# Dense attention of a six-phase model: norm roots for four token tiles at once, scaling by ScalarE, and the norm's bias times the weights by one-column products

## The chip, the cores and the metric

The kernel runs on one core of a Trainium2 chip. A core has five engines, each with an instruction queue of its own that it works off in order: TensorE (PE in the profile; its weight loads are listed apart as PEld), VectorE (DVE), ScalarE (ACT), GpSimd (POOL) and SyncE (SP), which here only issues transfers. The metric is device time in microseconds. The kernel before was run three times: 3253.14, 3248.87 and 3249.95 us, a median of 3249.95 us.

## The reference

The input `x` is fp32 of shape (4, 1024, 128). Six phases follow each other, each added to `x`: a feed-forward, an attention by squared distances, the same feed-forward again, a windowed block (two layers, each a 64-token windowed attention of 8 heads and a gated part), the dense attention, and the windowed block again with the same weights.

```python
x = x + 0.5 * ffn(layernorm(x))           # phase ffn0a
x = x + l2_attention(layernorm(x))        # phase attn0
x = x + 0.5 * ffn(layernorm(x))           # phase ffn0b
x = x + 0.5 * windowed(layernorm(x))      # phase ffn1a
x = x + dense_attention(layernorm(x))     # phase attn1
x = x + 0.5 * windowed(layernorm(x))      # phase ffn1b
```

The change touches the dense attention alone. With 16 heads of 64 it computes, for every batch of 1024 tokens:

```python
mu, var = mean(x), var(x)                           # over the 128 features
xn  = (x - mu) / sqrt(var + 1e-05) * gamma + beta
q, k, v = split(xn @ w_qkv.T)                       # w_qkv is (3072, 128), no bias of its own
sim  = (q * 64 ** -0.5) @ k.T                       # per head, entries above the diagonal masked
out  = softmax(sim) @ v
y    = concat_heads(out) @ w_out.T + b_out
```

`x` comes to it through the layer norm without parameters of the line above, and it normalises again inside; the two norms are computed as one, with both epsilons in one root.

`xn @ w_qkv.T` splits into two parts: the normalised tokens times weights that have gamma multiplied in, and a constant of each output column, the sum over the features of `beta[d] * w_qkv[e, d]`. These 3072 constants are called the norm's bias times the weights below. gamma and beta are drawn at random, so neither is trivial.

## The kernel before

**Planner.** The kernel is not written in the order in which it runs. Each phase is a function that records small steps, each a closure of one or a few instructions, by `at(t, f)` with a nominal time `t`. A class `Plan` finds the dependencies between steps from the buffers that they touch, prices every step with a cost table, and lists the steps of each engine in an order: at each point an engine takes, of the steps that could start now, the one with the smallest priority (`order`). Buffers in SBUF and PSUM are placed in the same pass, and a step that opens a buffer waits until a place is free. From the result it works out the latest time of each step (`latest`), uses these as new priorities, and keeps the best of six such passes (`best_order`). Then the instructions are emitted, and each engine executes its list strictly in that order. So an edit of a few steps can reorder the work of neighbouring phases. All instructions carry line 237, that of the helper that issues them (`issue`).

**Phases.** `tile_macaron` records the six phases; each starts near the end of the one before and overlaps with it by as much as the planner finds room for. `attn1` (line 1087) gets its nominal start `T0`, and its preparation starts 40 nominal us ahead (`lead`). The preparation overlaps with the end of the windowed block.

**Dense attention.** A head pair (two heads of 64, together 128 columns) of one batch is the unit: 4 batches by 8 pairs are 32 pairs, n = 8b + p, each nominally 30.9 us. Its parts are:

- `load`, `mask`, `gain`, `load2` (lines 1097 to 1111): gamma, beta, the causal mask, gamma times 1/8, the output weights and bias. Beta is read as a row that is broadcast to 128 partitions.
- `weights(t, k)` (line 1113): the 3072 columns come in six blocks of 512, in the order 2, 0, 4, 3, 1, 5 (0 and 1 queries, 2 and 3 keys, 4 and 5 values); the last three are recorded 30 nominal us later, and are first needed by pair 4. `fetch` loads a block with features on partitions (`raw`, two buffers). `high` (ScalarE) multiplies it by gamma and rounds it to fp32r; `low` (DVE) makes the rest that the rounding left. For the bias, `fetch_rows` loads the same 512 columns a second time with the columns on partitions (`nat`, 256 KB), `times_bias` (POOL) multiplies by beta, and `total` (DVE) sums over the features into four columns of `bias`; for queries a further DVE step multiplies by 1/8.
- `norm(t0, w, b, t)` (line 1149), for each of the 8 token tiles of 128 of a batch: `stats` (two DVE instructions: mean and variance), `var` (DVE), the helper `rsqrt` (line 608: an integer estimate of 1/sqrt and two refinements, eight DVE instructions, here on one column), `scale` (DVE, 128x128), `bias_x` (POOL adds the output bias to x), `turn` (TensorE transposes the tile into PSUM), `upper` (ScalarE copies and rounds to fp32r) and `lower` (DVE, the rest). The first batch's eight norms are recorded in the preparation, 1.5 nominal us apart; those of batch b+1 one per pair while batch b is worked on.
- `project`: query and key projections of a pair, in two halves of 512 tokens. Each is three matmuls into PSUM (high times high, high times low, low times high), a ScalarE copy that adds the bias column (`upper`), a DVE subtraction (`lower`), and transfers that spread the two heads over separate tiles.
- `value`: the values of one token tile for four pairs, three matmuls and a DVE copy.
- `heads`: scores (four PSUM banks, 0 to 3), maximum (DVE), exp with its sum (ScalarE), reciprocal (DVE), normalising (POOL), transposing (TensorE, banks 4 and 5) and copying.
- `weigh`: probabilities times values (bank 6), the copy that adds the value bias, the output projection, and the addition to x.

All norm transposes, projections, values and output projections share one PSUM bank, number 7, under the name `wide`: each of them has to wait until its predecessor there is read.

In phases ffn0a, attn0 and ffn0b a different norm helper is used, `norm4` (line 644): statistics of four tiles, one root for the four columns, and the scaling of chosen tiles by ScalarE.

Of the kernel before, what the change touches and what calls it, by code (L numbers as in the profile page):

```python
# [14 lines left out]
AF = mybir.ActivationFunctionType  # L15
ALU = mybir.AluOpType
AX = mybir.AxisListType
# [4 lines left out]
EPS = 1e-5  # L22
# [69 lines left out]
class Plan:  # L92
# [22 lines left out]
    def at(self, t, f, *args):  # L115
        self.steps.append(Step(t, f, args))
# [478 lines left out]
class Macaron:  # L595
# [491 lines left out]
    def attn1(self, ph, T0, lead):  # L1087

        V, at, pe, ac, ve, gp, sy, tile_ = self.begin("a1.")
        a, plan = self.a, self.plan  # L1090
        W = {}
        T = 30.9
        wide = lambda: plan.bank("a1.m", [7], turns=False)
# [3 lines left out]
        def load():  # L1097
            W["gam"], W["gam8"], W["bet"] = tile_([128, 1], "gam"), tile_([128, 1], "gam8"), tile_([128, 128], "bet")
            W["bias"], W["cm"] = tile_([128, 24], "bias"), tile_([128, 128], "cm", 1, BF)
            sy.dma_start(out=W["gam"], in_=a["L1_attn_ln_gamma"].unsqueeze(1))  # L1100
            sy.dma_start(out=W["bet"], in_=a["L1_attn_ln_beta"].unsqueeze(0).broadcast_to([128, 128]))

# [11 lines left out]
        def weights(t, k):  # L1114
# [13 lines left out]

            def fetch_rows():
                W["nat", k] = tile_([128, 4, 128], "nat", 2)  # L1130
                rows = a["L1_attn_w_qkv"].rearrange("(c p) d -> p c d", p=128)
                sy.dma_start(out=W["nat", k], in_=rows[:, 4 * k : 4 * k + 4, :])

            def times_bias():
                gp.tensor_tensor(W["nat", k], W["nat", k], W["bet"].unsqueeze(1).broadcast_to([128, 4, 128]), ALU.mult)

            def total():
                o = W["bias"][:, 4 * k : 4 * k + 4]
                ve.tensor_reduce(o, W["nat", k], AX.X, ALU.add)
                if k < 2:  # L1140
                    ve.tensor_scalar(o, o, 0.125, None, ALU.mult)

            at(t, fetch)
            at(t + 0.1, fetch_rows)
            for j, f in enumerate((high, low, times_bias, total)):
                at(t + 3 + 0.5 * j, f)


        def norm(t0, w, b, t):
            x = lambda: self.X[2 * b + t // 4][:, t % 4, :]  # L1150
            K = ("ln", b, t)
            cs = slice(128 * (t % 4), 128 * (t % 4) + 128)

            def stats():
                s6, mv = tile_([128, 6], "s6", 3), tile_([128, 2], "mv", 3)
                V[K] = mv, tile_([128, 1], "lv", 3), tile_([128, 1], "ly", 3)
                ve.bn_stats(s6, x())
                ve.bn_aggr(mv, s6)

            def var():  # L1160
                mv, v, y = V[K]
                ve.tensor_scalar(v, mv[:, 1:2], 1.0 + EPS, EPS * EPS, ALU.mult, ALU.add)

            def scale():
                mv, v, y = V[K]
                V["xn", K] = tile_([128, D], "xn", 3)
                ve.tensor_scalar(V["xn", K], x(), mv[:, 0:1], y, ALU.subtract, ALU.mult)

# [234 lines left out]
        for t in range(8):  # L1403
            norm(tb + 5 + 1.5 * t, 2.0, 0, t)
        for t in range(8):
            value(T0 - 6.0 + 0.7 * t, 0, 0, t)
        work = [2 * (3.3 * (i + 1) + 2) for i in range(8)]
        for n in range(N):
# [6 lines left out]
            if b + 1 < self.B:  # L1415
                norm(t0 - 21.0, 8.0, b + 1, p)
            if n + 4 < N:
# [668 lines left out]
```

## Time and profile before

| quantity | value |
|---|---|
| median of three runs | 3249.95 us |
| the profiled execution's own time | 3244.27 us |
| its span (first to last instruction) | 3242.3 us |
| instructions | 76442 |
| mean granted TensorE clock | 0.984 |
| PE busy | 3033.2 us, 94% |
| PEld busy | 2128.3 us, 66% |
| DVE busy | 2237.5 us, 69% |
| ACT busy | 2455.6 us, 76% |
| POOL busy | 1461.8 us, 45% |
| transfers | 138.96 MB in 212596 packets, mean 43 GB/s |
| chain that ended last | PE 54%, DVE 17%, ACT 17%, issue 6%, POOL 5%, DMA 1%, SP queue 1% |

"Busy" is the time in which an engine had an instruction running; neighbouring instructions can overlap, so that the sum of single durations is longer than the time that they take. The chain that ended last is followed back from the last instruction of the program: at each step to what released it, or to the instruction before it on its engine. The granted clock is the share of full speed that TensorE was given. Since all instructions carry one line, groups are told apart by engine, operation, the program's buffer names (`words` and `wordsS` in SBUF, `wordsR` rounded fp32r tiles in SBUF, `wordsP` in PSUM) and by shape.

A few events of the time around the changed code, in us from the span's start: the last scores of the windowed attention on TensorE 1343.2; the transfers of gamma and beta issued 1343.8; the statistics of the first token tile of the dense attention 1345.5; the transposes of its eight tiles 1353.6 to 1375.5; the first key projection 1390.7; the first query projection 1404.3; the first scores of the dense attention 1412.1; the last work of the dense attention about 2536.

### The profile page before, as it was taken

How to read it: one execution, taken by the hardware profiler on the slowest of the kernel's cores; microseconds unless marked ns; L12 is line 12 of the kernel's file. 1: busy time of each engine (PE TensorE's matmuls, PEld its weight loads, DVE VectorE, ACT ScalarE, POOL GpSimd, SP SyncE). 2: the span in 40 equal slices, each digit the busy share in tenths (PEclk: the TensorE clock that was granted, in tenths of full speed). 3: DMA queues.
4: the chain of work that ended last, by engine and by line, in shares of the span. 5: the costliest groups of instructions: out<-in, count | busy, mean ns of one | idle time of the engine just before them, and what ended most of it. 6: DMA issues, size and time to landing. Idle time of an engine off the chain costs nothing.

```text
span 3242.3 us, 76442 instructions
## 1 busy us (share of the span) xinstructions
PE 3033.2 (94%) x27033; PEld 2128.3 (66%) x27060; DVE 2237.5 (69%) x6889; ACT 2455.6 (76%) x6818; POOL 1461.8 (45%) x1627
## 2 busy tenths in 40 slices
PE   8999999989998999889999999999999899999988
PEld 6322222667776777667777777777777677777767
DVE  8433341568767676788888888887787787676774
ACT  6999999778868686647767766777777788686873
POOL 1000000179958585433333333333343799585870
PEclk9999999999999999989999999999999999999999
DMA  1000000022212121222222121222231322122211
GB/s 40 1 1 1 1 3 11 25 69 64 55 39 59 44 56 31 52 67 46 47 52 45 42 51 42 45 48 52 45 84 35 75 56 58 37 59 46 57 42 30
DMA packets 212596, 138.96 MB, mean 43 GB/s; under 512 B 148516, under 2 KB 167800, under 8 KB 212216
## 3 DMA queue, kind: packets, MB, share of 16 engines
q1 hardware_dynamic: 211496, 133.51, 18.1%
q8 instruction: 217, 3.56, 0.5%
q14 instruction: 163, 1.34, 0.1%
q0 software_dynamic: 720, 0.56, 0.1%
HBM read 19.22 MB, written 2.10 MB: 7 GB/s over the span
## 4 chain that ended last, share of the span: by engine, by line
PE 54%; DVE 17%; ACT 17%; issue 6%; POOL 5%; DMA 1%; SPq 1%; DVEq 0%; ACTq 0%; POOLq 0%
PE wordsP L237 54%; ACT wordsS L237 12%; DVE wordsS L237 11%; DVE words L237 4%; POOL wordsS L237 4%; ACT words L237 4%; POOL words L237 1%; DVE wordsP L237 1%; DVE wordsR L237 1%; SPq L237 1%; ACT wordsR L237 0%; DMA wordsS<-wordsS 0%; ACT wordsP L237 0%; DMA words<-W_vT 0%; DMA words<-words 0%
## 5 line engine op out<-in xcount | busy, mean ns | idle before, releaser
L237 PE MATMUL wordsP<-wordsS 128*128 128x128 f32 (+7 forms) x12013 | 1653.3, 330 | 131.6 <-POOL wordsS L237 48.7
L237 ACT ACTIVATE wordsS<-wordsP,wordsS 128x128 f32<-128x128 f32 (+4 forms) x1952 | 920.8, 495 | 349.8 <-PE wordsP L237 211.0
L237 PEld LDWEIGHTS wordsP<-wordsS 128*128 128x128 f32 (+3 forms) x10248 | 916.2, 144 | 356.2 <-POOL wordsS L237 101.8
L237 POOL TENSOR_SCALAR wordsS<-wordsS 128x128 f32<-128x128 f32 (+7 forms) x630 | 478.0, 761 | 686.3 <-DVE wordsS L237 489.0
L237 PE MATMUL wordsP<-wordsR 128*128 128x512 f32 (+2 forms) x2592 | 725.9, 411 | 20.1 <-DVE wordsR L237 5.9
L237 POOL TENSOR_TENSOR wordsS<-wordsS 128x512 f32<-128x512 f32 (+1 forms) x518 | 541.5, 1060 | 445.4 <-DVE wordsS L237 422.1
L237 ACT COPY wordsS<-wordsP 128x512 f32<-128x512 f32 (+4 forms) x1040 | 543.2, 540 | 188.1 <-PE wordsP L237 181.0
L237 DVE TENSOR_REDUCE wordsS<-wordsP 128x1 f32<-128x512 f32 (+4 forms) x1024 | 576.4, 581 | 75.3 <-PE wordsP L237 68.8
L237 PE MATMUL wordsP<-wordsS,words 128*64 128x64 f32 (+3 forms) x6216 | 521.3, 298 | 32.3 <-DVE words L237 12.6
L237 PEld LDWEIGHTS wordsP<-wordsR 128*128 128x128 f32 (+1 forms) x2592 | 454.7, 192 | 124.0 <-ACT words L237 10.2
L237 ACT ACTIVATE wordsS<-wordsP 128x1024 f32<-128x1024 f32 (+3 forms) x640 | 515.7, 869 | 25.1 <-PE wordsP L237 20.7
L237 PE MATMUL wordsP<-words 128*128 128x512 f32 (+3 forms) x1540 | 418.1, 376 | 11.9 <-DMA words<-W_vT 10.6
L237 ACT ACTIVATION_READ_ACCUMULATOR wordsS<-wordsP,wordsS 128x1 f32 x1792 | 397.5, 222 | 0.0
L237 DVE COPY wordsS<-wordsP 128x512 f32<-128x512 f32 (+4 forms) x444 | 238.6, 550 | 211.0 <-PE wordsP L237 206.2
L237 PEld LDWEIGHTS <-wordsS 64*128 64x128 bf16 (+1 forms) x1792 | 117.9, 95 | 389.3 <-issue 372.2
L237 PEld LDWEIGHTS wordsP<-wordsS,words 128*64 128x64 f32 (+2 forms) x5704 | 300.4, 136 | 99.1 <-issue 47.5
L237 DVE TENSOR_TENSOR wordsS<-wordsP,wordsS 128x256 f32<-128x256 f32 (+3 forms) x560 | 251.9, 461 | 160.7 <-PE wordsP L237 123.1
L237 DVE TENSOR_TENSOR words<-wordsP,wordsS 128x256 f32<-128x256 f32 (+1 forms) x448 | 227.3, 526 | 129.8 <-PE wordsP L237 83.9
L237 PEld LDWEIGHTS wordsP<-words 128*128 128x128 f32 x1540 | 247.7, 192 | 43.4 <-DMA words<-W_kT 10.6
L237 PEld LDWEIGHTS wordsP<-words,wordsS 64*64 64x64 f32 (+1 forms) x4672 | 186.6, 142 | 78.3 <-issue 54.6
L237 PE MATMUL wordsP<-words,wordsS 64*64 64x128 f32 (+1 forms) x4672 | 227.2, 279 | 7.7 <-POOL words L237 2.7
L237 ACT ACTIVATE words<-wordsP,wordsS 128x512 fp32r<-128x512 f32 (+1 forms) x192 | 131.2, 690 | 73.3 <-PE wordsP L237 66.3
(62 smaller groups left out, 2263.7 us busy)
## 6 DMA issues: line engine op xcount, KB each, us to landing
words<-words SPq DMA_DIRECT2D x648, 128.0 KB
wordsS<-words SPq DMA_DIRECT2D x88, 128.0 KB
wordsS<-wordsS SPq DMA_DIRECT2D x48, 128.0 KB
wordsS<-wordsS SPq DMA_DIRECT2D x48, 112.0 KB
wordsS<-c_rot SPq DMA_DIRECT2D x16, 256.0 KB
wordsS<-L_attn_x SPq DMA_DIRECT2D x8, 256.0 KB
words<-wordsS SPq DMA_DIRECT2D x16, 128.0 KB
out_dram<-wordsS SPq DMA_DIRECT2D x8, 256.0 KB
```

Of the source, the lines that this page charges most:

```text
L237: self.follow(engine, getattr(engine.engine, name)(*args, **kw))
```

## The change

It has two parts and a new place in the schedule for one of them.

**Bias.** Beta is loaded as one column, one feature per partition (512 bytes in place of a broadcast of 64 KB). `fetch_rows` and its 256 KB transfers, POOL's multiplication and DVE's sums are gone. In their place TensorE multiplies the block `raw` with the column of beta: four fp32 products per block with 128 columns of `raw` as weights and one column of result each, in PSUM bank 7. ScalarE copies the four columns into `bias` and multiplies those of queries by 1/8 on the way. These two steps are recorded ahead of `high` and `low`. `raw` is read once more, so it is held until the products are done.

**Norm.** `norm` is split into `stats` (per tile, now into one 128x4x2 buffer for four tiles), `root4` (variance, `rsqrt` on four columns, and a shift of minus mean times root) and the rest (`norm`), in which ScalarE scales the tile by Identity with the root as scale and the shift as bias.

**Schedule.** For the first batch, statistics stay 1.5 nominal us apart, and each root follows on the fourth of them. For later batches the statistics of all eight tiles are recorded in the first four pairs of the batch before, the roots at pairs 1 and 3, and the four scalings and transposes behind each root 6 nominal us apart.

Counted over the kernel, DVE gets 248 instructions fewer, POOL 6 fewer, SP 6 issues fewer; ScalarE gets 38 more (32 scalings, 6 copies) and TensorE 24 one-column fp32 products.

```diff
 def load():
-    W["gam"], W["gam8"], W["bet"] = tile_([128, 1], "gam"), tile_([128, 1], "gam8"), tile_([128, 128], "bet")
+    W["gam"], W["gam8"], W["bet"] = tile_([128, 1], "gam"), tile_([128, 1], "gam8"), tile_([128, 1], "bet")
     sy.dma_start(out=W["gam"], in_=a["L1_attn_ln_gamma"].unsqueeze(1))
-    sy.dma_start(out=W["bet"], in_=a["L1_attn_ln_beta"].unsqueeze(0).broadcast_to([128, 128]))
+    sy.dma_start(out=W["bet"], in_=a["L1_attn_ln_beta"].unsqueeze(1))
...
-    def fetch_rows():
-        W["nat", k] = tile_([128, 4, 128], "nat", 2)
-        rows = a["L1_attn_w_qkv"].rearrange("(c p) d -> p c d", p=128)
-        sy.dma_start(out=W["nat", k], in_=rows[:, 4 * k : 4 * k + 4, :])
     def times_bias():
-        gp.tensor_tensor(W["nat", k], W["nat", k], W["bet"].unsqueeze(1).broadcast_to([128, 4, 128]), ALU.mult)
-    def total():
-        o = W["bias"][:, 4 * k : 4 * k + 4]
-        ve.tensor_reduce(o, W["nat", k], AX.X, ALU.add)
-        if k < 2:
-            ve.tensor_scalar(o, o, 0.125, None, ALU.mult)
+        pb = W["pb", k] = wide()
+        for c in range(4):
+            pe.matmul(pb[:, c : c + 1], W["raw", k][:, 128 * c : 128 * c + 128], W["bet"], start=True, stop=True)
+    def keep_bias():
+        ac.activation(W["bias"][:, 4 * k : 4 * k + 4], W["pb", k][:, 0:4], AF.Copy, scale=0.125 if k < 2 else 1.0)
     at(t, fetch)
-    at(t + 0.1, fetch_rows)
-    for j, f in enumerate((high, low, times_bias, total)):
+    for j, f in enumerate((times_bias, keep_bias, high, low)):
         at(t + 3 + 0.5 * j, f)
...
+def root4(t0, w, b, q):
+    K = ("ln", b, q)
+    def get():
+        return V[K][1:3]
+    def var():
+        mv, v = V[K][:2]
+        ve.tensor_scalar(v, mv[:, :, 1], 1.0 + EPS, EPS * EPS, ALU.mult, ALU.add)
+    def shift():
+        mv, v, y, z = V[K]
+        ve.scalar_tensor_tensor(z, mv[:, :, 0], -1.0, y, ALU.mult, ALU.mult)
+    at(t0, var)
+    self.rsqrt(V, tile_, [t0 + (0.1 + 0.1 * j) * w for j in range(8)], get, K + ("r",))
+    at(t0 + 0.9 * w, shift)
+def stats(t0, b, t):
+    def f():
+        K = ("ln", b, t // 4)
+        if t % 4 == 0:
+            V[K] = tile_([128, 4, 2], "mv", 2), *(tile_([128, 4], "l" + z, 2) for z in "vyz")
+        s6 = tile_([128, 6], "s6", 3)
+        plan.await_place(V[K][0])
+        ve.bn_stats(s6, self.X[2 * b + t // 4][:, t % 4, :])
+        ve.bn_aggr(V[K][0][:, t % 4, :], s6)
+    at(t0, f)
 def norm(t0, w, b, t):
...
     def scale():
-        mv, v, y = V[K]
         V["xn", K] = tile_([128, D], "xn", 3)
-        ve.tensor_scalar(V["xn", K], x(), mv[:, 0:1], y, ALU.subtract, ALU.mult)
+        y, z = (c[:, t % 4 : t % 4 + 1] for c in V["ln", b, t // 4][2:])
+        ac.activation(V["xn", K], x(), AF.Identity, bias=z, scale=y)
...
-    at(t0, stats)
-    at(t0 + 0.1 * w, var)
-    self.rsqrt(V, tile_, [t0 + (0.2 + 0.1 * j) * w for j in range(8)], lambda: V[K][1:], K + ("r",))
-    at(t0 + 1.1 * w, scale)
-    at(t0 + 1.2 * w, bias_x)
-    at(t0 + 1.3 * w, turn)
-    at(t0 + 1.5 * w, upper)
-    at(t0 + 1.7 * w, lower)
+    at(t0, scale)
+    at(t0 + 0.1 * w, bias_x)
+    at(t0 + 0.2 * w, turn)
+    at(t0 + 0.4 * w, upper)
+    at(t0 + 0.6 * w, lower)
...
 for t in range(8):
-    norm(tb + 5 + 1.5 * t, 2.0, 0, t)
+    stats(tb + 5 + 1.5 * t, 0, t)
+    if t % 4 == 3:
+        root4(tb + 5.2 + 1.5 * t, 2.0, 0, t // 4)
+        for u in range(t - 3, t + 1):
+            norm(tb + 7.2 + 1.5 * t + 0.6 * (u % 4), 2.0, 0, u)
...
     if b + 1 < self.B:
-        norm(t0 - 21.0, 8.0, b + 1, p)
+        for u in range(2 * p, 2 * p + 2) if p < 4 else ():
+            stats(t0 - 21.0 + 8.0 * (u % 2), b + 1, u)
+        if p in (1, 3):
+            root4(t0 - 12.0, 4.0, b + 1, p // 2)
+            for u in range(4):
+                norm(t0 - 6.0 + 6.0 * u, 4.0, b + 1, 4 * (p // 2) + u)
```

More of the change, by code (lines that the diff above doesn't have):

```diff
@@ L1152, in norm @@
             cs = slice(128 * (t % 4), 128 * (t % 4) + 128)
[L1154 to L1160, printed above, removed]
-                mv, v, y = V[K]
-                ve.tensor_scalar(v, mv[:, 1:2], 1.0 + EPS, EPS * EPS, ALU.mult, ALU.add)
             def scale():
-                mv, v, y = V[K]
                 V["xn", K] = tile_([128, D], "xn", 3)
-                ve.tensor_scalar(V["xn", K], x(), mv[:, 0:1], y, ALU.subtract, ALU.mult)
+                y, z = (c[:, t % 4 : t % 4 + 1] for c in V["ln", b, t // 4][2:])
+                ac.activation(V["xn", K], x(), AF.Identity, bias=z, scale=y)
             def bias_x():
```

## Prediction

> **What bounds the kernel now.** I read the table of stages first, then the chain that ended last around the changed code, then waits and single groups there. The six phases lie one after another; the changed code is all in the dense attention, whose scores begin at 1412 us and whose work ends at about 2536 us, and in the 90 us before them, where the previous phase (windowed attention with its gated part) runs out while the dense attention's weights and first norms are made ready. I call those 90 us the ramp. The stages (columns: length, busy time of each engine with its instructions, granted TensorE clock, DMA share, GB/s):
>
> ```profile
> core 0: us, PE busy (x) PEld busy (x) DVE busy (x) ACT busy (x) POOL busy (x), PEclk, DMA share, GB/s
> 1344.00:1412.00 68.00, 51.47 (x340) 39.80 (x329) 62.49 (x252) 25.90 (x59) 22.31 (x31) 0.86 0.25 60
> 1412.00:1448.00 36.00, 35.67 (x223) 27.48 (x222) 29.30 (x95) 24.05 (x72) 12.24 (x17) 0.89 0.19 41
> 1448.00:2502.00 1054.00, 1035.20 (x7676) 790.96 (x7674) 859.89 (x2584) 756.39 (x2173) 380.87 (x520) 1.00 0.22 49
> ...
> 1381.00:1389.00 8.00, 7.45 (x22) 5.40 (x21) 6.90 (x19) 2.21 (x6) 5.29 (x9) 0.50 0.25 50
> ```
>
> The long stage belongs to TensorE: idle for 1054 - 1035.2 = 18.8 us in all. DVE work taken out there can win a part of 18.8 us and no more, and TensorE work put in there costs its full time. The ramp belongs to DVE: 62.5 us of 68, ScalarE 25.9. TensorE's work in the ramp, at full clock, is about 51.5 x 0.86 = 44 us, so at most 68 - 44 = 24 us can go from it. The groups of DVE in the ramp show what the change takes out (one-column root arithmetic, the 128x128 scaling, the sums of weights times bias):
>
> ```profile
> L237 DVE SCALAR_TENSOR_TENSOR wordsS<-wordsS 128x1 f32<-128x1 f32 x53 | 12.2, 240 | 0.0
> L237 DVE TENSOR_TENSOR wordsS<-wordsS 128x1 f32<-128x1 f32 x41 | 7.3, 185 | 0.0
> L237 DVE TENSOR_SCALAR wordsS<-wordsS 128x128 f32<-128x128 f32 x15 | 5.3, 366 | 0.1
> L237 DVE TENSOR_REDUCE wordsS<-wordsS 128x4 f32<-128x512 f32 x6 | 4.1, 677 | 0.0
> ```
>
> In the chain that ended last, the last 30 us of the ramp are a string of transfers and single products (start, length, what):
>
> ```profile
> 1384.68 2.87 DMA wordsS<-L_attn_w_qkv
> ...
> 1387.61 1.39 POOL wordsS L237
> ...
> 1393.83 3.17 DMA wordsS<-w_qkvT
> ...
> 1404.33 1.66 PE wordsP L237 x3
> ...
> 1411.09 1.66 PE wordsP L237 x3
> ...
> 1413.54 35.60 PE wordsP L237 x227
> ```
>
> From 1413.5 us it is TensorE without a break. ScalarE's timeline shows why the string is slow: in the same 12 us it twice stood still for weights that are needed only four head pairs later:
>
> ```profile
> 1397.09 0.72 ACT L237 ACTIVATE wordsR<-wordsS 128x512 fp32r<-128x512 f32 x1 [2.86 <-DMA wordsS<-w_qkvT]
> ...
> 1402.57 0.72 ACT L237 ACTIVATE wordsR<-wordsS 128x512 fp32r<-128x512 f32 x1 [3.57 <-DMA wordsS<-w_qkvT]
> ```
>
> **The change part by part.** The sum is made against the profiled execution, 3244.27 us (span 3242.3); the median of the runs is 3249.95, 5.7 above it, and I carry a difference over unchanged.
>
> 1. *Work taken from DVE.* 32 tiles times 10 operations (variance, eight of the root, scaling) and 8 for the weights' sums are replaced by 8 groups times 10: 248 instructions fewer. In the ramp DVE does 14 tiles' roots; the listed groups and 4.2 us of other one-column steps make 33 us by busy time. Neighbours overlap by about half, so it is 16 to 33 us less 4 groups x 10 x 0.15 us = 6 put in: 10 to 27 us of DVE. Of that the path sees only what it waited for.
>
> 2. *Six products on POOL, six row transfers of 256 KB and a 64 KB broadcast go.* POOL's two first products, 1347.7 to 1350.2 us, held two root steps of DVE at 1.21 and 1.22 us where the same step takes 0.15 otherwise: 2 x 1.06 = 2.1 us on the chain. On SP's queue the six issues (about 0.4 us each) go from between the others, the weights' fetches included. The Trainium skill, "SBUF — State Buffer", section "Who interferes with whom", says that a DVE instruction with two SBUF inputs is blocked for the whole of a GpSimd instruction that reads SBUF; the trace agrees (1.21 against 0.15 us). By that rule all six products would each have held one DVE step, 6 x 1.06 = 6.4 us of DVE in place of 2.1.
>
> 3. *Products with one column.* 24 fp32 matmuls, each two instructions. The nearest row is the gated part's bias, `128*114 128x1`: 24 instructions are 2.8 us busy, 0.117 each, and they start 0.10 apart. So 8 x 0.10 = 0.8 us for each of six weight blocks: three in the ramp (hidden in TensorE's 16.5 idle us or worth up to 2.4 us), three after the first scores, where TensorE never waits: +2.4 us in full. Each holds the one PSUM bank of the dense attention (bank 7) until ScalarE has copied four columns, about 0.2 us, behind whatever is ahead in ScalarE's queue.
>
> 4. *Scaling on ScalarE.* 32 x 0.48 us (the same form, 128x128 with two pointers, is 484 ns in the earlier phases) against 0.37 on DVE. ScalarE is 38% busy in the ramp and 72% in the long stage, so I cost it at nothing; without that cover the eight first would cost 8 x 0.48 = 3.9 us. What waits behind such an instruction is every later ScalarE step: gelus in the ramp, exps later (rival C).
>
> 5. *The order.* The kernel's planner orders everything anew from 1318 us to the end of the dense attention; before and behind that the orders agree. I walk the new order with the old durations.
>  a. 1318 to 1338 us: gamma and beta now lie where a table frees early, so their load no longer waits for the last local scores (it was issued at 1343.8 us); POOL's products for the exps come ahead of an addition, so a TensorE wait of 3.6 us (to 1322.99) should close. But the gain of gamma now stands ahead of the statistics on DVE, and two weight roundings ahead of eight exps on ScalarE, all behind gamma's transfer. Bounds: -3.6 us, and +3 (two 0.75 us DVE steps and as much waiting). I take -1, nearer the loss.
>  b. To the last transpositions of the windowed attention's output (1381.4 us): TensorE's own sequence carries it: 0.8 x 3 more products, two transposes earlier, and less waiting for DVE (1.07, 1.43, 0.68 and part of a 2.47 us gap). Net -1; between +2.4 and -5.
>  c. From there to the first scores: 1412.1 - 1381.4 = 30.7 us now. In the new order the values of five tiles are already done, the norm of the next batch and one late weight block no longer stand in bank 7's way, and the key and query projections sit between the last gated products. At full clock: 1.8 us until the first key projection, 6.8 us of products to the second (0.7 for three of 512 columns, 0.66 for six of 128 by the start-to-start spacing), then its copy 0.7, the issue of two key copies and a weight fetch 1.8, that transfer 3.2, rounding 0.7, query copy 0.7, subtraction 0.75, second query 0.7 + 0.7, DVE's queue and subtraction 2, a value product 0.7: 21 us, so -10. The lower bound on the gain is a half clock as in 1381 to 1389 us (0.50): about 4 us back, -6.
>  d. When scores begin, two more value products are behind (2 x 0.7): -1.4.
>
> 6. *Long stage.* DVE loses some 17 tiles' roots, about 17 x 1.5 = 26 us of 860; TensorE's wait on DVE here is 9.8 of its 18.8 us. A tenth of that, -1; bounds -8 and +5, since a new order can make as many small waits as it removes.
>
> Sum: -1 - 1 - 10 - 1.4 + 2.4 - 1 = -12. I take two off for semaphore steps that the walk leaves out: -10, 3234 for a profiled run, 3240 by the median. No change means within 0.2%, 6.5 us.
>
> **The rivals.**
> A. *The ramp gains half.* Fetches of two late weight blocks still stand on SP behind the copies of the second key projection, and their roundings ahead of both query copies on ScalarE. If both old waits come back in full (2.86 + 3.57 = 6.4 us), c gives -4 and the whole -4: 3246. For it: ScalarE's order; against: the fetches go out together, so the second wait is shared, and I have counted one.
> B. *More.* If step a closes its whole 3.6 us, DVE's relief takes 4 us from the long stage, and no half clock comes: -10 - 2.6 - 3 = about -16, 3234.
> C. *Slower by ScalarE's queue.* In the long stage 24 scalings in six groups wait for a chain of ten dependent DVE steps of about 0.2 us, 2 us in all, and every exp behind them waits too; four score banks cover TensorE for about as long as four score products, 2 us. If DVE, 82% busy there, lags its place by another 3 us each time, six groups cost 18 us: -10 + 18 = +8, 3258. It decides from 1.7 us a group, where the gain is gone. For it: ScalarE takes its steps in order. Against: ScalarE is idle 28% of that stage, and the scalings are placed after the root. The Trainium skill, "ScalarE: Activation LUTs", section "Rules for kernel authors", puts multiplies and adds on VectorE. In durations the trace agrees (0.48 against 0.37 us), but here the freer engine gets the work.
> D. *It does not do what it says:* the roots are off the path and nothing moves. The chain has DVE in most of its pieces from 1346 to 1372 us; I give it the rest within 0.2%.
>
> **How the numbers follow.** Forecast (-6.5 to -14) 0.47; B 0.15; A 0.24; D and offsets 0.05; C 0.09. Faster 0.62, within 0.2% 0.29, slower 0.09. From -21 (B with the rest of b) to +1 (A with step a lost) leaves out about 0.15: 3229 to 3251.
>
> **What would show it.** After: DVE under 55 us busy between the same ramp events; the first score 8 to 14 us earlier; no row transfers; 48 one-column products of 0.10 us spacing; TensorE's idle time in the long stage within 5 us of 18.8. Wrong, if ScalarE waits for DVE before each group of scalings in the long stage, if gamma's transfer holds ScalarE near 1330 us, or if the query copies wait over 5 us for weights.

## The result, and the profile after

The changed kernel takes 3223.18 us (median of five runs, 3219.09 to 3224.32); the kernel before, in five runs, 3250.48 us. The ratio is 0.9914 with a 95% interval of 0.9903 to 0.9926: 27 us faster, where 10 us were forecast. The direction was right, the size was not, and the time lies below the range of 3229 to 3251. All times below are medians of fast runs; one slow run each of cut_late (4576 us), pad_late (5856 us) and order_b2 (10139 us) is left out.

The profiled execution has a span of 3217.8 us against 3242.3. I cut both traces at the same events: the scores of one tile late in the windowed attention (about 1240 us), the first scores of the dense attention, the first scores of its pair 24 (from there on no norm of a later batch is left to do), and the last work of TensorE. In this and the later tables, the *ramp* is the stretch from the first of these events to the second, the *long stage* from the second to the third.

| | before | after | difference |
|---|---|---|---|
| up to the windowed scores | 1239.2 | 1240.7 | +1.5 |
| ramp | 172.9 | 161.3 | -11.6 |
| long stage | 833.9 | 816.3 | -17.6 |
| from pair 24 to the dense attention's last output projection | 271.1 | 271.1 | 0.0 |
| from there to TensorE's end | 719.5 | 723.2 | +3.7 |

The last row has the same work in both; in the profiles of this study it takes 718 to 725 us, so its 3.7 us are scatter. The ramp was forecast about right: the prediction's -1, -1 and -10 for it add up to -12. The long stage, for which the prediction's terms added up to nothing, gave most of the gain.

The stages of the changed kernel, cut as in the prediction (length, busy time of each engine with its instructions, granted clock, DMA share, GB/s):

```profile
core 0: us, PE busy (x) PEld busy (x) DVE busy (x) ACT busy (x) POOL busy (x), PEclk, DMA share, GB/s
1344.00:1402.00 58.00, 51.20 (x404) 41.87 (x405) 44.33 (x150) 29.61 (x72) 13.52 (x23) 0.97 0.20 46
1402.00:1438.00 36.00, 35.97 (x248) 29.05 (x247) 27.14 (x79) 25.42 (x77) 12.94 (x18) 0.94 0.21 49
1438.00:2474.00 1036.00, 1028.88 (x7671) 789.89 (x7671) 831.93 (x2451) 764.02 (x2194) 378.58 (x519) 1.00 0.22 50
1382.00:1390.00 8.00, 7.28 (x43) 5.92 (x44) 4.70 (x12) 2.99 (x7) 3.50 (x7) 1.00 0.30 58
```

VectorE's 62.5 us in the ramp became 44.3. In the long stage TensorE was idle for 18.8 us; now it is 1036 - 1028.9 = 7.1 us. And its busy time fell by 6 us with about as many instructions (7676 and 7671), at a granted clock of 1.00 in both. The half clock from 1381 to 1389 us did not come back.

The groups of VectorE in the ramp now hold root arithmetic on four columns:

```profile
L237 DVE SCALAR_TENSOR_TENSOR wordsS<-wordsS 128x4 f32<-128x4 f32 x24 | 4.2, 187 | 0.3
L237 DVE TENSOR_TENSOR wordsS<-wordsS 128x4 f32<-128x4 f32 x15 | 3.1, 212 | 0.2
L237 DVE TENSOR_SCALAR wordsS<-wordsS 128x128 f32<-128x128 f32 x3 | 0.9, 342 | 0.0
```

The end of the ramp in the chain that ended last (start, length, what): one weight transfer stands in it where there were two, and no GpSimd product.

```profile
1383.82 7.18 PE wordsP L237 x42
...
1391.02 0.70 ACT words L237
...
1392.88 3.17 DMA wordsS<-w_qkvT
...
1396.14 0.73 ACT wordsR L237
...
1397.56 0.74 DVE words L237
...
1400.88 16.98 PE wordsP L237 x100
```

In ScalarE's timeline the two stops for late weights became one, as the prediction's walk had counted (rival A would have had both):

```profile
1396.14 0.72 ACT L237 ACTIVATE wordsR<-wordsS 128x512 fp32r<-128x512 f32 x1 [3.72 <-DMA wordsS<-w_qkvT]
1397.33 0.71 ACT L237 ACTIVATE wordsR<-wordsS 128x512 fp32r<-128x512 f32 x1
```

And where the long stage's time went shows in TensorE's waits between the first scores and pair 24. Before (engine and tiles, what it waited for: us in total, times, longest):

```profile
PE wordsP L237 <- DVE wordsS L237: 8.1, 12, 1.1
PE wordsP L237 <- POOL wordsS L237: 4.8, 10, 1.0
PE wordsP L237 <- ACT wordsS L237: 1.7, 4, 0.7
PE wordsP L237 <- DVE words L237: 1.3, 4, 0.4
```

After:

```profile
PE wordsP L237 <- POOL wordsS L237: 3.5, 8, 0.7
PE wordsP L237 <- ACT wordsS L237: 0.7, 3, 0.3
PE wordsP L237 <- DVE wordsS L237: 0.7, 2, 0.4
PE wordsP L237 <- DVE words L237: 0.2, 1, 0.2
```

Of 9.4 us of waits for VectorE 0.9 are left. The prediction had taken a tenth of them to go; nine tenths went.

### The profile page after: what moved, and what is told of

The parts are those of the page before. It is cut to its first block, busy times and chain, and to the rows that moved or that the text cites. A ratio compares the mean times of both kernels' runs of the same rounds, so it can differ in the third digit from the quotient of the medians.

```text
span 3217.8 us, 76341 instructions
## 1 busy us (share of the span) xinstructions
PE 3029.4 (94%) x27082; PEld 2134.7 (66%) x27108; DVE 2192.4 (68%) x6641; ACT 2467.9 (77%) x6856; POOL 1451.3 (45%) x1621
## 4 chain that ended last, share of the span: by engine, by line
PE 58%; ACT 16%; DVE 13%; issue 5%; POOL 5%; DMA 1%; SPq 1%; DVEq 0%; ACTq 0%; POOLq 0%
PE wordsP L237 58%; ACT wordsS L237 12%; DVE wordsS L237 8%; POOL wordsS L237 3%; ACT words L237 3%; DVE words L237 3%; POOL words L237 1%; SPq L237 1%; DVE wordsP L237 1%; DVE wordsR L237 1%; DMA wordsS<-wordsS 1%; ACT wordsR L237 0%; DMA words<-words 0%; ACT wordsP L237 0%; DMA wordsS<-L_attn_x 0%
## 5 line engine op out<-in xcount | busy, mean ns | idle before, releaser
L237 PE MATMUL wordsP<-wordsS 128*128 128x128 f32 (+8 forms) x12062 | 1657.9, 331 | 114.2 <-POOL wordsS L237 44.1
L237 PEld LDWEIGHTS wordsP<-wordsS 128*128 128x128 f32 (+3 forms) x10296 | 926.0, 145 | 329.4 <-POOL wordsS L237 85.3
L237 PE MATMUL wordsP<-wordsR 128*128 128x512 f32 (+2 forms) x2592 | 718.9, 409 | 13.6 <-ACT words L237 4.1
L237 POOL TENSOR_TENSOR wordsS<-wordsS 128x512 f32<-128x512 f32 (+1 forms) x512 | 532.6, 1053 | 430.2 <-DVE wordsS L237 411.4
L237 ACT COPY wordsS<-wordsP 128x512 f32<-128x512 f32 (+4 forms) x1040 | 543.8, 541 | 170.6 <-PE wordsP L237 160.7
```

The costliest lines, as they stand in the source:

```text
L237: self.follow(engine, getattr(engine.engine, name)(*args, **kw))
```

## The experiments

Two things had to be told apart: the work that the change moves, and the order in which the planner lists everything once the work has changed. In some kernels the planner sees the old work (or the new), so that every engine's order stays as it was, and instructions are left out or added only when the list is emitted (`plan.recording` is false then). These say what work is worth in a fixed order. In others the planner orders anew.

### Parts of the change alone

**norm_only** has the norm's part with the old bias, **bias_only** the one-column products with the old norm; both are ordered anew.

> The norm's part of the change alone (roots for four tiles, scaling on ScalarE, the new schedule) with the bias as in the kernel before; the planner orders anew. Theories 1 and 2: the long stage keeps its gain of about 17 us and is 2.4 us better without the products; in the ramp half of the 10 us remains: 3221 to 3231. Theory 3: the long stage is as before, only the ramp gains: 3242 to 3248.

> The bias part of the change alone (one-column products) with the norm as in the kernel before; the planner orders anew. Theories 1 and 2: the long stage is 0 to 3 us longer, since three blocks' products of 0.8 us stand in it, and the ramp gains 2 to 6 us: 3243 to 3251. Theory 3: 3228 to 3236.

| | median us | ratio to before, 95% | ramp | long stage |
|---|---|---|---|---|
| before | 3250.48 | | 172.9 | 833.9 |
| norm_only | 3221.25 | 0.9912 [0.9897, 0.9927] | 160.8 | 818.3 |
| bias_only | 3243.30 | 0.9979 [0.9970, 0.9988] | 160.7 | 839.2 |
| after | 3223.18 | 0.9914 [0.9903, 0.9926] | 161.3 | 816.3 |

The norm alone is as fast as the whole change, and the long stage's gain comes with the norm's part. Either part alone makes the ramp 12 us shorter, and both together no more than one: the ramp's gain is not a sum of works saved. That much was expected of neither (5 us for the norm, 2 to 6 for the bias). The bias part loses 5.3 us in the long stage, and more than that in its first pair (39.9 us against 32.8): three blocks' products take 2.4 us there, and two more products of three matmuls on rounded tiles (33 of these matmuls against 27), left over from the ramp, 2.0. Ahead of its first scores it still stood for transfers of the first pair's queries and keys, the largest single wait in TensorE's list, in a ramp that was 12 us shorter nevertheless:

```profile
PE wordsP L237 <- DVE wordsS L237: 7.8, 11, 1.1
PE wordsP L237 <- DMA words<-words: 5.8, 1, 5.8
```

### VectorE's work taken out in the old order

**cut_late**: the order of before; the norms of the three later batches issue only the estimate of the root.

```diff
 for t, f in zip(times, (y0, sq, tv, p1, p2, sq, n1, n2)):
-    at(t, f)
+    at(t, f if f is y0 else unless_cut(f))   # for b > 0, f is recorded and planned, not emitted
```

**cutall_late** goes further: variance and all eight steps are left out, and ScalarE copies the tile in the place where VectorE scaled it.

> The kernel before with its order of steps kept as it is on every engine; for the norms of the three later batches seven of the eight root instructions on VectorE are not issued (168 instructions of one column fewer, all in the long stage; the roots stay rough estimates, so the numbers of these batches differ). Theory 1, VectorE's load: the 17.6 us that the long stage lost come from VectorE's root work being gone, which let maxima and reciprocals of the softmax start earlier. Then -10 to -17 here: 3233 to 3240. Theory 2, the order: they come from the new order (roots and transposes grouped by four, done earlier), and the work alone is worth at most 3 us: 3247 to 3251. Theory 3, the bias: they come from the missing sums, GpSimd products and row transfers: no change, 3249 to 3252.

> The kernel before with its order kept on every engine; the 24 norms of the later batches issue no root at all (variance and eight root steps left out), and ScalarE copies the tile where VectorE scaled it, so these batches are not normalised. VectorE then has 240 instructions fewer in the long stage, as many as in the changed kernel. Leaving out 168 of them gave 11.6 us of the 17.6. Theory 1a, VectorE's load is all of it: 15 to 18 us from the first scores to pair 24, 3229 to 3235 in all. Theory 1b, load is two thirds and the new order the rest: 11 to 13 us, 3236 to 3239. Rival, ScalarE's queue: scalings in the places of the old order delay exps, and the gain falls below 10 us: over 3240.

cut_late: 3237.25 us, ratio 0.9958 [0.9941, 0.9975]; ramp 172.6 us as before, long stage 821.9, so -12.0 us. cutall_late: 3237.96 us, 0.9969 [0.9956, 0.9981], long stage 822.5, so -11.4. So leaving out root steps of VectorE wins two thirds of the 17.6 us without any change of order; leaving out the scaling too gives nothing besides in this order. The waits of TensorE in cut_late are nearly those of the changed kernel:

```profile
PE wordsP L237 <- POOL wordsS L237: 4.5, 10, 0.7
PE wordsP L237 <- ACT wordsS L237: 1.7, 4, 0.6
PE wordsP L237 <- DVE wordsS L237: 1.3, 3, 0.6
PE wordsP L237 <- DVE words L237: 0.2, 1, 0.2
```

One of the waits that went, in detail. Before, TensorE's timeline shows it standing for 1.09 us until VectorE was done:

```profile
1623.98 0.63 PE L237 MATMUL wordsP<-wordsS 128*128 128x128 f32 x4 [1.09 <-DVE wordsS L237]
```

VectorE's timeline of the kernel before in the stretch ahead of it:

```profile
1621.49 0.16 DVE L237 RECIPROCAL wordsS<-wordsS 128x1 f32<-128x1 f32 x1
1621.57 1.60 DVE L237 SCALAR_TENSOR_TENSOR wordsS<-wordsS 128x1 f32<-128x1 f32 x2
1623.21 0.16 DVE L237 TENSOR_TENSOR wordsS<-wordsS 128x1 f32<-128x1 f32 x1
1623.29 0.55 DVE L237 COPY wordsS<-wordsP 128x384 f32<-128x384 f32 x1
```

and GpSimd's, which normalises two rows of probabilities:

```profile
1620.94 2.23 POOL L237 TENSOR_SCALAR wordsS<-wordsS 128x1024 f32<-128x1024 f32 x2 [3.29 <-PE wordsP L237]
```

The copy at 1623.29 empties the PSUM bank that TensorE's next transposes need. Ahead of it stand two root steps on one column, for a norm that is needed many us later. Together they take 1.60 us, and the second ends at 1623.17, where GpSimd's instruction ends. In cut_late VectorE's timeline has nothing between the reciprocal and the copy; VectorE even waits for TensorE there:

```profile
1618.28 0.16 DVE L237 RECIPROCAL wordsS<-wordsS 128x1 f32<-128x1 f32 x1
1618.91 0.56 DVE L237 COPY wordsS<-wordsP 128x384 f32<-128x384 f32 x1 [0.47 <-PE wordsP L237]
```

Over the long stage of the kernel before, 29 of 202 steps of root arithmetic took over 0.3 us; these 29 make 20.9 us of their 47.2. All 29 have two inputs, and each ends within 0.06 us of the end of a GpSimd instruction; none of the 51 steps with one input took over 0.2 us. TensorE stood over 0.25 us 27 times, and in 10 of these (7.3 of 15.3 us) such a stretched step had begun in the 3 us ahead. In the changed kernel it is 15 of 76 steps, and one of 10 waits (0.3 us). Five of these 15 have one input and four columns (up to 0.96 us, again ending with a GpSimd instruction), so it is only on one column that one input was seen to be safe.

### VectorE's work given back in the new order

**pad_late** adds ten instructions behind each later tile's statistics, **pad_even** one product of two one-column inputs behind 8 of a pair's 24 maxima; **scale_dve** puts the 24 later scalings back on VectorE. All keep the changed kernel's order.

```diff
 # pad_late, in stats, b > 0
+for j in range(9):
+    ve.scalar_tensor_tensor(s6[:, 0:1], s6[:, 0:1], -0.5, s6[:, 1:2], ALU.mult, ALU.mult)
+ve.tensor_reduce(s6[:, 2:3], x, AX.X, ALU.max)
 # pad_even, in top, z == 0 and i % 2 and n < 22
+ve.tensor_tensor(V["m", K, k][1][:, 0:1], W["bias"][:, 0:1], W["bias"][:, 1:2], ALU.mult)
 # scale_dve, b > 0
-ac.activation(V["xn", K], x(), AF.Identity, bias=z, scale=y)
+ve.tensor_scalar(V["xn", K], x(), y, z, ALU.mult, ALU.add)
```

> The changed kernel with its order kept as it is on every engine; behind the statistics of each of the 24 tiles of the three later batches ten VectorE instructions are issued in addition (nine dependent ones of one column, one reduction over 128 columns; they write scratch columns only). That gives VectorE back about as much work as the change took from it in the long stage. Theory 1: the long stage gets longer again by 10 to 17 us: 3233 to 3240. Theory 2: at most 4 us longer, 3223 to 3227. Theory 3: likewise at most 4 us longer.

> The changed kernel with its order kept on every engine; behind 8 of the 24 maxima of each of the pairs 0 to 21 one VectorE product of one column is issued in addition (176 in all, independent of each other, written to a column that the exp's sum overwrites later). This gives back VectorE's load evenly, where the first padding stood in lumps of up to 10 us. Theory 1 (load): the long stage gets 8 to 14 us longer, 3231 to 3238. Rival (only chains and lumps of dependent root steps cost time, single instructions find gaps): at most 4 us longer, 3222 to 3227.

> The changed kernel with its order kept on every engine; the 24 scalings of the later batches are issued on VectorE again (24 x 0.41 us = 10 us of its 30 us saved). By its share of the load: the long stage 3 to 6 us longer than 816.2. By the run in which taking the scaling off VectorE besides the roots gave nothing more (822.5 against 821.9): within 1.5 us.

pad_late: 3284.05 us, 1.0106 [1.0086, 1.0126], long stage 858.3 us, +42. Nobody expected that, and it is no measure of load: in the new order the statistics of four tiles stand side by side, so the padding made blocks of up to 40 instructions, and TensorE waited once 8.2 and once 7.5 us for VectorE. Its granted clock was 0.97 over that stage, where the changed kernel has 1.00; how much of the 42 us this is was not separated. pad_even: 3234.73 us, 0.9958 [0.9943, 0.9972], long stage 829.6, +13.3: about as many us as leaving the steps out had won. scale_dve: 3229.43 us, one run, long stage 822.3, +6.1. So in the new order the scalings' place matters, where in the old order cutall_late had found them free; why the two differ was not followed.

### Amount or collision

The last two kernels keep the number of added instructions and take away the second input. **one_input** is cut_late with each missing step replaced by a plain product with a constant; **pad_one** is pad_even with a constant.

```diff
 # one_input: for each root step that cut_late left out
+ve.tensor_scalar(t, y, 0.125, None, ALU.mult)
 # pad_one, in place of the tensor_tensor of pad_even
+ve.tensor_scalar(V["m", K, k][1][:, 0:1], W["bias"][:, 0:1], 0.125, None, ALU.mult)
```

> The kernel before with its order kept; for the 24 norms of the later batches the seven root steps behind the estimate are issued as seven plain products of one column with a constant, one input each (the roots stay rough estimates). The number of VectorE instructions is that of the kernel before, 168 more than where they were left out. Theory 1c, collisions: it is root steps with two inputs, stretched from 0.16 to about 1 us while GpSimd normalises (29 of 202 steps in the kernel before, 20.9 of their 47.2 us), that make VectorE's copies and reciprocals late. Then most of the gain stays: the long stage 822 to 827 us. Theory 1d, number and length of the steps: the long stage is back at 830 to 834 us.

> The changed kernel with its order kept; the 176 evenly spread one-column instructions of the earlier run, now with one input and a constant in place of two inputs. With two inputs (0.243 us each) the long stage was 829.6 us in place of 816.3. Theory 1c: 818 to 823 us. Theory 1d: 826 to 830 us.

| | added on VectorE, one column | ns each | median us | ratio, 95% | long stage |
|---|---|---|---|---|---|
| before | root steps, two inputs | 253 and 282 | 3250.48 | | 833.9 |
| cut_late | none | | 3237.25 | 0.9958 [0.9941, 0.9975] | 821.9 |
| one_input | 168, one input | 147 | 3237.33 | 0.9967 [0.9951, 0.9982] | 821.7 |
| after | none | | 3223.18 | 0.9914 [0.9903, 0.9926] | 816.3 |
| pad_even | 176, two inputs | 243 | 3234.73 | 0.9958 [0.9943, 0.9972] | 829.6 |
| pad_one | 176, one input | 145 | 3224.07 | 0.9917 [0.9895, 0.9940] | 820.0 |

The long stages of cut_late and one_input, whose stage rows agree in all but VectorE's instructions:

```profile
1412.00:2233.90 821.90, 812.38 (x5975) 620.76 (x5973) 661.64 (x1969) 589.10 (x1697) 292.61 (x403) 1.00 0.21 48
```

```profile
1411.70:2233.40 821.70, 812.28 (x5975) 620.69 (x5973) 675.26 (x2099) 589.71 (x1697) 294.04 (x403) 1.00 0.21 48
```

130 instructions and 13.6 us of VectorE's time more in that window cost nothing. The groups of the padding in pad_even, and in pad_one (which holds a dozen steps of the norm besides), show the only difference between +13.3 and +3.8 us:

```profile
L237 DVE TENSOR_TENSOR wordsS<-wordsS 128x1 f32<-128x1 f32 x176 | 42.8, 243 | 0.2
```

```profile
L237 DVE TENSOR_SCALAR wordsS<-wordsS 128x1 f32<-128x1 f32 x188 | 26.4, 145 | 0.2
```

So what the root steps cost the long stage in the old order was not their amount. It was that a step with two inputs, met by GpSimd's normalising, stands for up to 1 us in front of copies and reciprocals that TensorE needs soon. This is the rule that the prediction had cited from the Trainium skill, "SBUF — State Buffer", section "Who interferes with whom": a VectorE instruction with two SBUF inputs contends with a GpSimd instruction that reads SBUF, one with a single input (outside some fast modes) does not. Both halves agree with these runs on one column, 0.243 against 0.145 us; whether the four-column steps that were held run in one of those modes, no run here shows. The prediction applied it to GpSimd's six products alone, and not to the 24 norms beside GpSimd's normalising.

Two things qualify the comparison. The replacements in one_input do not depend on each other as root steps do; that dependence is not the cause is shown by pad_even and pad_one alone, whose steps are independent in both. And pad_one keeps 3.8 of the 13.3 us, of which about 1.9 go with a longer half clock (8.2 us of its long stage, 8.4 in pad_even, 4.5 in the changed kernel).

### The ramp

**cutall_ramp** leaves out the first batch's roots in the old order and copies its tiles on ScalarE; **no_products** leaves out GpSimd's six products of the bias.

> The kernel before with its order kept on every engine; the eight norms of the first batch issue no root, and ScalarE copies the tile where VectorE scaled it (the first batch is not normalised). If VectorE's roots in the ramp hold up the first scores by themselves, these come 4 to 8 us earlier than 1412 us; if the string of weight transfers and single products behind them sets the end, by less than 2 us.

> The kernel before with its order kept on every engine; GpSimd's six products of weights and beta are not issued (the bias is then the plain sum of the weights). The prediction counted 2.1 us for two root steps of VectorE that these products held up: first scores 1 to 2.5 us earlier than 1412.1. Rival: VectorE's roots are not what the first scores wait for (leaving them out gave 1.3 us), so under 0.7 us.

cutall_ramp: 3247.24 us, ramp 169.2, -3.8; its first scores stand only 1.3 us earlier than before, since it was 2.4 us late at the windowed scores. no_products: 3241.87 us, ramp 166.8, -6.1. Both are single runs.

The 6.1 us are not the price of the products alone. TensorE works off the same list in both kernels, so its instructions can be compared one by one. Between 1350 and 1377 us it gains 2.1 us, as the prediction had counted for two held steps. A third root step of VectorE, which took 1.24 us at 1376.86 beside a third product, makes 1.25 us more (TensorE's wait to 1379.97 falls from 2.47 to 1.22 us). The next 3.3 us come up to 1389 us, where the kernel before runs at the half clock and no_products at the full one; the same eight matmuls, before and in no_products:

```profile
1383.80 3.76 PE L237 MATMUL wordsP<-wordsR 128*114 128x512 f32 x8 [0.20 <-DVE wordsR L237]
```

```profile
1380.16 2.11 PE L237 MATMUL wordsP<-wordsR 128*114 128x512 f32 x8 [0.55 <-DVE wordsR L237]
```

Of this 0.4 us is lost again before the first scores. That no_products comes near the 6.4 us of the prediction's other sum is therefore chance. Why the clock stayed full there is open. Neither run makes 11.6 us. (The four profiles with the old order and all of the ramp's work have 172.5 to 172.9 us. Of the five with the changed kernel's order four have 161.3 to 164.3; pad_late, whose padding reaches into the ramp, has 180.1.)

### The order by itself

Seven kernels change only what the planner is told.

```diff
 # order_before, order_b2: later norms of the kernel before 3 us earlier, 1.5 us later
-norm(t0 - 21.0, 8.0, b + 1, p)
+norm(t0 - 24.0, 8.0, b + 1, p)      # order_b2: t0 - 19.5
 # order_b3: kernel before
-T = 30.9
+T = 31.3
 # order_a1, order_a2: changed kernel, statistics, roots, scalings 3 us earlier, later
 # passes_before, passes_after: either kernel, these steps 3 us later, and
-TRIES = 6
+TRIES = 10
-T = 30.9
+T = 30.5
```

> The kernel before with all its work; only the nominal time of the later batches' norms is 3 us earlier, so that the planner finds another order (2936 of TensorE's 19194 steps stand elsewhere). It tells how much a new order by itself moves the time. If orders scatter little (theory 1), the long stage stays within 4 us of the 833.9 us from the first scores to pair 24; if the 17.6 us were luck of the order, it moves by over 8 us either way.

> The kernel before with all its work, the later norms recorded 1.5 us later: one more order of the old work. If the old work's orders scatter by 10 us and more around a mean well below 3250 us (the kernel before had an unlucky one): 3234 to 3246. If the two faster orders so far were exceptions: 3247 to 3253.

> The kernel before with all its work, a nominal pair of 31.3 us in place of 30.9: another order. As for the one before: 3234 to 3246 if orders scatter, 3247 to 3253 if not.

> The changed kernel with statistics, roots and scalings of the later batches recorded 3 us earlier: another order of the new work. If VectorE's relief of 12 us in the long stage holds in any order and the ramp's 10 us were a lucky order: 3226 to 3238. If both hold in any order: 3220 to 3226.

> The changed kernel with the same steps recorded 3 us later: another order of the new work. 3226 to 3238 if the ramp's gain was a lucky order, 3220 to 3226 if it comes with the change.

> The kernel before with all its work; the planner only gets ten passes in place of six, a nominal pair of 30.5 us in place of 30.9, and the later norms 3 us later, a combination that its own costs like. If the ramp's 10 us are a matter of the order (the nudged order gave 9.8 us there without any change of work), a good order of the old work reaches first scores at 1400 to 1405 us; the long stage keeps VectorE's full load, so it gains no more than 4 us on 833.9: 3234 to 3241. If the order can make up for the load as well, 3222 to 3230, as fast as the changed kernel.

> The changed kernel with the same three settings of the planner. If the changed kernel's order was an average one, this is 3 to 10 us faster: 3213 to 3220. If it was already a lucky one, no change or up to 5 us slower: 3221 to 3228. The long stage has at most about 6 us of TensorE's idle time left to give.

The ratios are to the kernel before in the same series of runs.

| work | order | us | ramp | long stage |
|---|---|---|---|---|
| old | before | 3250.5 | 172.9 | 833.9 |
| old | order_before (one run) | 3237.0 | 162.5 | 831.8 |
| old | order_b2 | 3242.25, 0.9983 [0.9972, 0.9995] | 165.2 | 831.4 |
| old | order_b3 | 3249.3, 0.9991 [0.9972, 1.0010] | 175.0 | 833.1 |
| new | after | 3223.2 | 161.3 | 816.3 |
| new | order_a1 | 3230.5, 0.9942 [0.9919, 0.9964] | 167.1 | 821.4 |
| new | order_a2 | 3223.1, 0.9923 [0.9894, 0.9952] | 161.3 | 818.6 |

The ramp is 162 to 175 us with the old work and 161 to 167 with the new: a nominal time moved by 3 us, with no work changed, won 10.4 us of ramp. In these seven the long stage keeps apart: 831 to 834 with the old work, 816 to 821 with the new. The means are 832.6 and 818.8, a difference of 13.8 us, near the 12.0 and 13.3 of the runs with a fixed order.

The two kernels with ten passes do not fit this. The old work takes 3233.7 us there (0.9952 [0.9935, 0.9968]), the new 3227.7 (0.9935 [0.9921, 0.9950]). Their orders already differ ahead of 1240 us, by 14 us, so their stages up to the first scores can't be set beside the others. The long stage can: TensorE has the same number of instructions in it. Before, and passes_before:

```profile
1412.10:2246.00 833.90, 815.99 (x5975) 621.99 (x5973) 688.95 (x2099) 590.39 (x1697) 293.96 (x403) 1.00 0.21 47
```

```profile
1425.40:2241.80 816.40, 807.92 (x5975) 620.75 (x5976) 691.14 (x2131) 592.84 (x1700) 294.82 (x406) 1.00 0.21 47
```

With all its root steps the old work takes 816.4 us in this order, as in the changed kernel. Its steps are held as before (28 of 221 took over 0.3 us, 19.7 us together), but TensorE waits 4.2 us for VectorE in place of 9.4. Up to 3.9 of the 17.5 us are the half clock, in which the kernel before spends the first 7.8 us of its long stage and passes_before none. In passes_after the long stage is 814.5 us, 2 less. So the price of a held step depends on the order in which other work stands around it. With these settings the change is worth 6 us by the medians, with overlapping intervals, and not 27. What was expected of passes_before was wrong in both stages (first scores at 1400 to 1405, long stage at most 4 us shorter): the first scores came at 1425.4 and the long stage was 17.5 us shorter, and the two errors nearly cancelled in the time, which lies just below the range. Which of the three settings does it was not followed.

The old kernel won 14 us by these settings (3248.05 in the same series); the new one, 0.9935 in place of 0.9914, gave up about 7 by the medians. No kernel of the study is shown to be faster than the changed one; norm_only and order_a2 can't be told from it.

## Why the prediction was right or wrong

- **5c, the end of the ramp (-10): right.** From the late transpositions of the windowed attention (1381.0 before, 1382.0 after) to the first scores it is 31.1 us before and 20.0 after; the walk gave 21. It was right for the reason given, the order: order_before, which has all the old work, needs 23.6 us there, and bias_only 24.6. The walk also assumed the full clock, and met it: before, TensorE worked 8.7 us between 1378.9 and 1389.2 us at a granted clock of 0.50, which makes about 4 of the 11 us. That this order comes with the change was luck of the planner and not shown by anything in the edit.
- **5a (-1): the sign was wrong, by 2 us.** From the windowed scores at 1240 us to the last ones, 104.0 us became 104.9. The wait of TensorE for GpSimd to 1322.99 closed as foreseen, from 3.6 to 0.15 us. But two waits for ScalarE came in behind it (1.6 and 0.8 us), and the one for VectorE after them grew from 6.4 to 7.7; in between ScalarE stood 2.0 and VectorE 3.2 us for gamma, near 1330 us. The bounds of -3.6 and +3 held it.
- **5b (-1): right**, 37.9 us became 36.4. **5d (two value products fewer behind the first scores): right**, three of them: the first pair's matmuls on rounded 512-column tiles went from 27 to 18.
- **2, GpSimd's products (2.1): right for the two steps counted, and one overlooked.** A third root step was held for 1.24 us at 1376.86 (and a fourth for 0.67 us at 1407.40). Some 3 of no_products' 6.1 us go with the clock.
- **3, one-column products (0.8 a block): right**, 0.81 to 0.93 us a block, from its first product to the next instruction on TensorE.
- **4 and rival C: ScalarE's queue did not become a bound.** Its waits for VectorE in the long stage fell, as ScalarE's rows before and after show:

```profile
ACT wordsS L237 <- DVE wordsS L237: 32.1, 44, 4.0
```

```profile
ACT wordsS L237 <- DVE wordsS L237: 27.3, 46, 2.1
```

- **The long stage, 5d, 3 and 6 together (-1.4 + 2.4 - 1 = 0): wrong, -17.6.** The step that failed is 6: "A tenth of that, -1". The row was there, 9.8 us of waits for VectorE, and the choice of a tenth had no row behind it. Even its bound of -8 was too near, since it took idle time as all that can go; 5.9 of the 17.6 us were inside TensorE's busy time, some 1.5 of them by a shorter half clock at its start (4.5 us in place of 7.8). cut_late, with the same matmuls, also wins 3.6 us there, 1.4 of them by the clock: matmuls that count as busy hold waits too. In the old order cut_late puts 12.0 us on root steps alone, and one_input and the paddings show that it was their second input. The prediction had the price of one collision, 1.06 us, but looked for it only in the ramp. The other 5.6 us lie within what orders of the new work differ by (816.3 to 821.4). What stays open is whether the changed kernel needed fewer steps for its 816.3 us, or only an order in which they are not in the way: passes_before has 816.4 with all of them.
- **"Wrong, if"**: of the three signs named, gamma's transfer held ScalarE near 1330 us, at the small price above; the other two did not come. TensorE's idle time in the long stage left its 18.8 us by 11.7 where 5 were allowed, on the good side.
- Rival B had the right direction, with 4 us from VectorE's relief where it was 12 in the old order.

## What to carry to other kernels

Cost a small instruction by what it can collide with and by who stands behind it in its queue, not by its length: a one-column step of 0.16 us took 1 us beside a GpSimd instruction, and in front of a PSUM copy that was TensorE's wait. In another order the old work, with as many held steps, had a long stage within 2 us of the new work's. A busy engine's idle time is no upper bound for what relief of another engine can win, because waits hide in busy time too. Before a saving is put down to work left out, look whether the granted clock was the same: about half of no_products' gain went with the clock. And where a planner orders the work, compare several orders of the old and of the new work: a nudge without any change of work moved this kernel by 11 us (3237.0 against 3247.8 in the same series), two fifths of what the change won, and another order of the old work reached the changed kernel's long stage.

## What the hardware showed unexpectedly

VectorE instructions on one column with a single input took 0.145 and 0.147 us on average with GpSimd busy for a third of the time; with two inputs 0.243 to 0.282. In a fixed order, 168 single-input instructions more in the long stage changed it by 0.2 us, and root steps with two inputs in the same places by 12. One input was not enough on four columns: such a step took up to 0.96 us beside GpSimd.
